# Four graph layers in one kernel: x W of layer 1 in halves, a different order at the first layer change, and other ends for layers 1 to 3

## The chip, the cores and the metric

The kernel runs on one core of a Trainium2 chip. The metric is the device time in microseconds (us), the median of several runs. The core has five engines with a queue each: TensorE (PE; its weight loads are shown as PEld), VectorE (DVE), ScalarE (ACT), GpSimd (POOL) and SyncE (SP), which here only issues transfers. An engine executes its queue in order and waits on semaphores.

## The reference

There are 4096 nodes, 256 features and a dense adjacency of 4096 x 4096 floats, of which most entries are zero. Each layer is followed by a residual sum and a layer norm over the features (LN).

```python
# layer 0: four heads of 64, masked where adj == 0
qkv = x @ Wqkv + bqkv
scores = q k^T / 8 + graph_bias * adj; masked to -1e9 where adj == 0
x = LN(x + (softmax(scores) @ v) @ Wout + bout)
# layer 1: one head, additive scores
Wh = x @ W;  e = leaky_relu((Wh @ a[:256])[:, None] + (Wh @ a[256:])[None, :], 0.2)
x = LN(x + softmax(e where adj > 0 or on the diagonal) @ Wh)
# layer 2
A = d[:, None] * adj * d[None, :]        # d = rowsum(adj) ** -0.5
x = LN(x + (A @ x) @ W2.T + b2)
# layer 3
x = LN(x + relu(A @ x @ W3))
```

## The kernel before, in words

A node block is 128 rows (a chunk, `NCH` = 32 of them); `xc` holds all chunks' rows, `mv` and `rstd` their mean, variance and reciprocal deviation. The order of instructions is written out by hand: `tc.manual_schedule()` keeps on each engine the order in which the program names them, and waits between engines follow from what each reads and writes.

**Layer 0** works in steps of 1024 columns; 64 units (32 row blocks by two head pairs) of 4 steps. Lists of what else is done in a step are kept in `plan` and `tail`. In the last steps the rows of layer 0's output, written to `x0_pre`, are loaded again in eight *parts* of four chunks (`load_part`), normalised (`norm_part`), written to `x0`, and turned into `turned_x` (`turn_part`). Parts 6 and 7 contain the last chunks and are turned last. `project_ed` makes from all turned parts the key scores `ed_b`. `project_w` (L132) multiplies a part with W and with W a: two halves, each 8 matmuls into one of the two double banks `sc[0]`, `sc[1]` of PSUM and one ScalarE copy into `store` (`wh`). The column next to Wh is the node's query score: `take_es` gathers it into `esd` on VectorE, and `spread_es` sends it through TensorE with a selecting matrix and back into `es_q`. At the end of layer 0 parts 0 and 1 are projected before parts 6 and 7 are turned.

**Layer 1** has 32 units (row blocks) of `NSB` = 4 passes of 32 rows, with the columns in four quarters over the partitions. `gat_step(t)` (L829) issues pass t of several stages: VectorE masks the edges (`mk`) and adds the key scores with a running maximum (`score`, L744 and L746), ScalarE adds the query score with the leaky slope (`leaky`, L759). When a unit's four maxima are there, ScalarE gathers them to one partition group (`gather_max`, L766), VectorE folds them (`fold_max`, L771), ScalarE spreads them (`spread_max`, L785). Then ScalarE takes the exponential (`expo`, L788), VectorE transposes (`turn`, L795), and TensorE multiplies with Wh (`attend`, L805): unit 0's `attend` starts in step 10 and needs all four turned passes of the unit. `finish` (L813) divides, adds to the row in `xc` and takes the statistics. In steps 0 to 5 each step also projects one of the parts 2 to 7; after that, in step 5, it takes and spreads the query scores of parts 2 to 7 and issues the eight loads of `xc`. SP's queue holds, in order, the edge masks of units 0 and 1, these eight loads, and the masks of unit 2 and later.

**Layers 2 and 3** multiply with the adjacency by a two-by-two scheme of seven products (Strassen's form). A step takes a pair of chunks c and c + 16 and a block of 512 columns from both halves: 7 products of 128 x 512 (L983), into seven PSUM banks `m0` to `m6`, accumulated over 16 steps; an eighth bank is tagged `y`. There are 4 column blocks a layer, so 128 steps. `load` (L938) brings two tiles of the adjacency by SP three steps ahead (4 buffers of two tiles); `sums` (L949) makes five sums or differences of them on VectorE one step ahead; `prepare` (L913) scales a pair's rows and makes five sums of them, during layer 2's first block, two steps ahead; layer 2's bias is added to the row by GpSimd there. After a block `keep` copies the seven banks out, `combine` makes four blocks of them, and `rows` (L1010) multiplies with W2 or W3, adds to `xc` and takes statistics, spread over later steps. `store` normalises the last layer's rows and writes the output. The end of the last block does all of this at once after the last product. Before layer 2's first step come `ln_rstd(0, NCH)`, `prepare(0, 0)` and `sums(0)`, which need the last unit's statistics.

## Time and profile before

| what | value |
| --- | --- |
| median of 3 runs (lowest, highest) | 2735.09 us (2731.63, 2736.67) |
| the profiled execution, its own time | 2734.35 us |
| its span | 2732.6 us |
| granted TensorE clock, mean | 0.992 |
| busy share of the span: PE, DVE, ACT, POOL | 98%, 80%, 60%, 14% |
| layer 1's last attend ends, layer 2's first product starts | 1875.3, 1881.5 us |
| adjacency load in layers 2 and 3, issue to landing, shortest, median, longest | 4.0, 5.1, 7.3 us |

A timeline row gives start, length, engine, line, operation and tiles, the number of instructions merged, and in brackets the engine's idle time before it with what released it; "issue" there means no releaser is shown. The same instruction can stand as two records: one product of 128 x 512 floats is two records of TensorE. Rows of stretches give, after the bounds and the length, the busy time of PE, PEld, DVE, ACT and POOL with the number of instructions, the granted clock (1.00 is full), the transfer engines' busy share and GB/s.

### The profile page before, as it was taken

How to read it: one execution, taken by the hardware profiler on the slowest of the kernel's cores; microseconds unless marked ns; L12 is line 12 of the kernel's file. 1: busy time of each engine (PE TensorE's matmuls, PEld its weight loads, DVE VectorE, ACT ScalarE, POOL GpSimd, SP SyncE). 2: the span in 40 equal slices, each digit the busy share in tenths (PEclk: the TensorE clock that was granted, in tenths of full speed). 3: DMA queues.
4: the chain of work that ended last, by engine and by line, in shares of the span. 5: the costliest groups of instructions: out<-in, count | busy, mean ns of one | idle time of the engine just before them, and what ended most of it. 6: DMA issues, size and time to landing. Idle time of an engine off the chain costs nothing.

```text
span 2732.6 us, 58953 instructions
## 1 busy us (share of the span) xinstructions
PE 2677.8 (98%) x23824; PEld 1836.4 (67%) x23824; DVE 2183.5 (80%) x3995; ACT 1647.8 (60%) x2675; POOL 379.4 (14%) x660
## 2 busy tenths in 40 slices
PE   8999999999999999999979999999999999999997
PEld 4777777777777777777768888885444444444443
DVE  4999999999999989999758888885866577676575
ACT  2899999999999999999857777771100001000000
POOL 1222232222222222223200000001200000000000
PEclk9999999999999999999999999999999999999998
DMA  6444444444444444444452222204554554555552
GB/s 146 94 96 96 89 94 95 92 96 94 88 96 95 92 90 96 97 89 91 143 160 73 77 78 77 74 20 133 179 159 155 174 159 153 168 175 161 183 174 69
DMA packets 679489, 312.35 MB, mean 114 GB/s; under 512 B 553520, under 2 KB 583600, under 8 KB 679216
## 3 DMA queue, kind: packets, MB, share of 16 engines
q1 hardware_dynamic: 655776, 265.10, 39.5%
q0 software_dynamic: 21632, 42.05, 4.3%
q8 instruction: 186, 3.05, 0.5%
q10 hardware_dynamic: 1808, 1.44, 0.2%
q14 instruction: 87, 0.71, 0.1%
HBM read 262.41 MB, written 46.07 MB: 113 GB/s over the span
## 4 chain that ended last, share of the span: by engine, by line
PE 94%; DVE 2%; DMA 2%; issue 1%; ACT 1%; SPq 0%; POOL 0%; DVEq 0%; POOLq 0%; ACTq 0%
PE m L983 28%; PE po L431 17%; PE sc L374 16%; PE po L805 16%; PE ptr L413 11%; PE py L1017 2%; PE pp L343 1%; PE pq L321 1%; PE pv L232 1%; PE pk L212 1%; DMA xt<-in_xT 0%; DMA mk<-edge 0%; DMA norm<-lt 0%; DMA x<-xs 0%; SPq L731 0%
## 5 line engine op out<-in xcount | busy, mean ns | idle before, releaser
L383 DVE CUSTOM_DVE_ANT_0 z<-sc,bias 128x1024 f32<-128x1024 f32 x512 | 606.0, 1221 | 50.9 <-PE sc L374 50.8
L399 ACT ACTIVATE z<-z,nm 128x1024 f32<-128x1024 f32 x512 | 590.6, 1154 | 0.0
L421 ACT COPY pt<-ptr 128x1024 f32<-128x1024 f32 x507 | 510.3, 1007 | 66.5 <-PE ptr L413 65.4
L431 PE MATMUL po<-pt,xc 128*64 128x128 f32 x8192 | 504.0, 276 | 0.0
L374 PE MATMUL sc<-store,qT 64*128 64x512 f32 x2048 | 502.9, 604 | 0.1
L805 PE MATMUL po<-store,pt 128*128 128x257 f32 x2048 | 447.2, 380 | 12.6 <-issue 12.6
L431 PEld LDWEIGHTS po<-pt,xc 128*64 128x64 f32 x8192 | 442.1, 137 | 17.5 <-DVE pt L419 0.2
L413 PEld LDWEIGHTS ptr<-ident,z 64*128 64x128 f32 x8192 | 322.9, 138 | 181.0 <-issue 86.9
L805 PEld LDWEIGHTS po<-store,pt 128*128 128x128 f32 x2048 | 389.1, 190 | 70.5 <-issue 12.7
L983 PE MATMUL m<-asum,ysum 128*128 128x512 f32 x768 | 356.7, 594 | 6.3 <-issue 6.3
L413 PE MATMUL ptr<-ident,z 64*128 64x64 f32 x8192 | 356.7, 225 | 5.1 <-ACT pt L421 3.7
L374 PEld LDWEIGHTS sc<-store,qT 64*128 64x128 f32 x2048 | 193.9, 189 | 115.6 <-issue 109.5
L983 PEld LDWEIGHTS m<-asum,ysum 128*128 128x128 f32 x768 | 146.2, 191 | 177.7 <-issue 160.8
L983 PE MATMUL m<-asum,store 128*128 128x512 f32 x512 | 263.3, 596 | 0.0
L983 PE MATMUL m<-a,ysum 128*128 128x512 f32 x512 | 246.0, 594 | 0.0
L989 ACT COPY e<-m 128x512 f32<-128x512 f32 x32 | 18.5, 585 | 351.3 <-PE m L983 351.3
L301 POOL DMA_DIRECT2D edge<-mk x256 | 143.1, 559 | 558.8 <-ACT mk L295 541.8
L759 ACT ACTIVATE z<-z,es_q 128x1024 f32<-128x1024 f32 x128 | 146.6, 1145 | 120.4 <-DVE mx L746 112.0
L952 DVE TENSOR_TENSOR asum<-a 128x512 f32<-128x512 f32 x128 | 88.0, 688 | 163.9 <-PE m L983 163.9
L284 DVE SCALAR_TENSOR_TENSOR bias<-rt,gb,u 128x512 f32<-128x512 f32 x256 | 194.2, 759 | 9.1
L795 DVE STREAM_TRANSPOSE pt<-z 128x1024 f32<-128x1024 f32 x128 | 158.0, 1236 | 41.7 <-PE po L805 41.7
L983 PEld LDWEIGHTS m<-asum,store 128*128 128x128 f32 x512 | 97.9, 191 | 123.2 <-issue 121.3
(122 smaller groups left out, 2601.3 us busy)
## 6 DMA issues: line engine op xcount, KB each, us to landing
a<-in_adjT SPq DMA_DIRECT2D x256, 512.0 KB, 5.1
raw<-in_adjT SPq DMA_DIRECT2D x512, 128.0 KB, 3.9
edge<-mk POOLq DMA_DIRECT2D x256, 128.0 KB, 2.4
mk<-edge SPq DMA_DIRECT2D x256, 128.0 KB, 2.9
xt<-in_xT SPq DMA_DIRECT2D x8, 512.0 KB, 5.1
xq<-in_xT SPq DMA_DIRECT2D x32, 128.0 KB, 3.6
xr<-in_x SPq DMA_DIRECT2D x32, 128.0 KB, 3.0
rb<-norm POOLq DMA_DIRECT2D x128, 32.0 KB, 2.4
```

Source lines behind the costliest of these rows:

```text
L284: nc.vector.scalar_tensor_tensor(self.bias[k][:, m0 : m0 + HT], rt, gb, u, ALU.mult, ALU.add)
L301: nc.gpsimd.dma_start(edge[self.ib * P : (self.ib + 1) * P, k * TS + m0 : k * TS + m0 + HT], mk)
L374: nc.tensor.matmul(ps[j][:, q * 512 : (q + 1) * 512], self.rows.qT[j * HD : (j + 1) * HD, self.pr, :], kT[j * HD : (j + 1) * HD, self.pr, ...
L383: nc.vector.tensor_tensor_reduce(z, ps[j], self.rows.bias[k], 1.0, NEG, ALU.add, ALU.max, self.mx[:, j, k : k + 1],)
L399: nc.scalar.activation(z, z, AF.Exp, bias=self.nm[:, j : j + 1], accum_out=self.ls[:, j, k : k + 1],)
L413: nc.tensor.transpose(pa[:, r, c, :], z[half, c * P : (c + 1) * P], ident[half, half])
L421: nc.scalar.copy(to, pa)
L431: nc.tensor.matmul(self.po[j * HD : (j + 1) * HD, 0:P], v_sb[:, ci, h * HD : (h + 1) * HD], self.pt[j][k][:, c, :], start=(ci == 0), stop= ...
L759: nc.scalar.activation(self.z[s], self.z[s], AF.Prelu, bias=self.eq[:, s : s + 1], alpha=SLOPE)
L795: nc.vector.transpose(self.pt[:, :, s, :], self.z[s].rearrange("p (b r) -> p b r", r=QB))
L805: nc.tensor.matmul(self.po[:, 0 : D + 1], self.pt[:, b, :, :].rearrange("p s i -> p (s i)"), wh[:, b, :], start=(b == 0), stop=(b == NBK - 1),
L983: nc.tensor.matmul(self.m[i], left, right, start=(c == 0), stop=(c == NP - 1))
```

## The change

**Between layers 0 and 1.** At the end of layer 0 only part 0 is projected before parts 6 and 7 are turned, and only its query scores are taken and spread. `project_w` now does one half, into a place it is given: `sc[0]`, `sc[1]` or `pm`, a third PSUM place. The fourteen other halves stand in steps 2 to 8 of layer 1, two or so a step; part 1's query scores are taken in step 2, those of parts 2 to 7 in step 9, the `xc` loads still in step 5. `leaky` comes two steps later, so that in ScalarE's queue a unit's gather comes before later leaky passes.

**Between layers 1 and 2.** The mask tiles' pool `bp` (7 tiles of 4 KB a partition) lives on and serves as the adjacency's buffers: two separate tiles a step. The loads of steps 0 to 2 are issued in the last steps of layer 1. The weights of layers 2 and 3 are loaded by SP in step 12 instead of by ScalarE. Chunks 0 to 30 are scaled, and pairs 0 and 1 prepared, into tiles of their own (`y_e`, `ysum_e`), six steps after the last pass's score; chunk 31's scale comes after the sums of step 0. The PSUM pool of layers 2 and 3 takes over its banks tile by tile.

**Steps of layers 2 and 3.** The products come in the order 2, 3, 0, 1, 4, 5, 6; products 2 and 3 read the adjacency tiles themselves, no sum. The difference that was one instruction over both tiles is two. The load for step t + 3 is issued after step t's second product.

**The end.** The last two steps are issued by product, both steps of a product together, in the order 2, 4, 0, 3, 6, 1, 5; blocks are combined in between, partly straight out of PSUM; rows are weighed from several banks; additions are shared between GpSimd and VectorE; and the output goes out in four transfers of two chunks.

```diff
-    def project_w(j):
-        xt = turned_x.pop(j)
-        for i in range(2):
-            pw = sc[i].rearrange("p (b e) -> p b e", b=2)
-            for b in range(2):
-                for cc in range(2):
-                    nc.tensor.matmul(
-                        pw[:, b, 0 : D + 1],
-                        xt[:, cc, 2 * i + b, :, :].rearrange("p a r -> p (a r)"),
-                        w_sb[:, cc, :],
-                        start=(cc == 0),
-                        stop=(cc == 1),
-                    )
-            bk = j * NSB + 2 * i
-            nc.scalar.copy(wh[:, bk : bk + 2, :], pw[:, :, 0 : D + 1])
+    def project_w(j, i, pw):
+        xt = turned_x[j] if i == 0 else turned_x.pop(j)
+        pw = pw.rearrange("p (b e) -> p b e", b=2)
+        for b in range(2):
+            for cc in range(2):
+                nc.tensor.matmul(
+                    pw[:, b, 0 : D + 1],
+                    xt[:, cc, 2 * i + b, :, :].rearrange("p a r -> p (a r)"),
+                    w_sb[:, cc, :],
+                    start=(cc == 0),
+                    stop=(cc == 1),
+                )
+        bk = j * NSB + 2 * i
+        nc.scalar.copy(wh[:, bk : bk + 2, :], pw[:, :, 0 : D + 1])
...
-            spread_es(0, 2 * NSB, ps_o.tile([P, 512], F32, tag="po0", name="pe"))
+            take_es(0, NSB)
+            spread_es(0, NSB, ps_o.tile([P, 512], F32, tag="po0", name="pe"))
...
                 (last_rstd,),
-                (project_w, 0),
-                (project_w, 1),
+                (project_w, 0, 0, sc[0]),
+                (project_w, 0, 1, sc[1]),
                 (norm_part, 6, NA - 1, NA),
                 (norm_part, 7, NA - 1, NA),
                 (turn_part, 6, True),
                 (turn_part, 7, True),
                 (project_ed, 6, NJ),
-                (take_es, 0, 2 * NSB),
                 (first_es,),
...
+    def load_last_weights():
+        nc.sync.dma_start(w2_sb, w2T.rearrange("(c p) e -> p c e", p=P))
+        nc.sync.dma_start(b2_b, b2.partition_broadcast(P))
+        nc.sync.dma_start(w3_sb, w3.rearrange("(c p) e -> p c e", p=P))
...
+    def prepare(p, layer):
+        dv = d2 if layer == 0 else d3
+        y, s = y_of(p), ysum_of(p)
+        for h in range(2):
+            ci = h * NP + p
+            ln_apply(xc[:, ci, :], xc[:, ci, :], ci)
+            nc.scalar.activation(y[:, h, :], xc[:, ci, :], AF.Copy, scale=dv[:, ci : ci + 1])
+            if layer == 0:
+                nc.gpsimd.tensor_tensor(xc[:, ci, :], xc[:, ci, :], b2_b, ALU.add)
+        nc.vector.tensor_tensor(
+            s[:, 1:3, :].rearrange("p a d -> p (a d)"), y[:, 0, :], y[:, 1, :], ALU.subtract
+        )
+        nc.vector.tensor_tensor(s[:, 3:5, :], y[:, :, 0:P], y[:, :, P : 2 * P], ALU.add)
+        nc.vector.tensor_tensor(s[:, 0, :], y[:, 0, 0:P], y[:, 1, P : 2 * P], ALU.add)
+    adj_t = {}
+    adj_s = {}
+    def load(t):
+        jb, c = divmod(t % T1, NP)
+        adj_t[t] = []
+        for k in range(2):
+            a = bp.tile([P, 2, BJ], F32, tag="bias", name=f"a{k}")
+            m0 = (k * NP + c) * P
+            nc.sync.dma_start(
+                a,
+                adjT[m0 : m0 + P, :].rearrange("p (h j i) -> p h j i", h=2, i=BJ)[:, :, jb, :],
+            )
+            adj_t[t].append(a)
...
-            u, s = at(t)
+            u, s = at(t - 2)
             if u:
                 u.leaky(s)
...
+        def more_es(j0, j1):
+            take_es(j0 * NSB, j1 * NSB)
+            spread_es(j0 * NSB, j1 * NSB, pm[:, 0:512])
...
+        filling = {}
+        halves = [(j, i) for j in range(1, NJ) for i in range(2)]
+        for t, n in ((2, 2), (3, 1), (4, 2), (5, 2), (6, 2), (7, 2), (8, 3)):
+            for _ in range(n):
+                j, i = halves.pop(0)
+                place = (sc[0], sc[1], pm)[(2 * j + i) % 3]
+                filling.setdefault(t, []).append((project_w, j, i, place))
+        filling[2].append((more_es, 1, 2))
+        filling[5].append((load_rows,))
+        filling[9] = [(more_es, 2, NJ), (degrees,)]
         with tc.manual_schedule():
             for t in range(n_t + NSB + 8):
                 gat_step(t)
-                if t + 2 < NJ:
-                    project_w(t + 2)
-                if t + 3 == NJ:
-                    take_es(2 * NSB, NBK)
-                    spread_es(2 * NSB, NBK, ps_o.tile([P, 512], F32, tag="pm", name="pe"))
-                    for j in range(NJ):
-                        nc.sync.dma_start(
-                            xc.rearrange("p (a j) e -> p a j e", j=NJ)[:, :, j, :],
-                            x0.rearrange("(a j p) e -> p a j e", p=P, j=NJ)[:, :, j, :],
-                        )
-                    nc.vector.reciprocal(d3, d3)
-                    nc.vector.reciprocal(d2, d2)
-                    nc.vector.tensor_scalar(sel, sel, -1.0, 1.0, ALU.mult, ALU.add)
-                    nc.vector.tensor_tensor(d2, d2, sel, ALU.mult)
+                if t == NJ + NSB:
+                    load_last_weights()
+                if n_t <= t < n_t + 3:
+                    load(t - n_t)
+                if t == n_t + NSB + 2:
+                    ln_rstd(0, NCH - 1)
+                    for p in range(NE):
+                        prepare(p, 0)
+                for f, *args in filling.get(t, ()):
+                    f(*args)
...
+        ps_m = l2.enter_context(
+            tc.tile_pool(name="l2ps_m", bufs=1, space=PSUM, reuse_waits="tile")
+        )
...
+            a0, a1 = adj_t[t]
             s = sp_.tile([P, 5, BJ], F32, tag="asum", name="asum")
-            nc.vector.tensor_tensor(s[:, 4, :], a[:, 0, 0, :], a[:, 1, 1, :], ALU.add)
-            nc.vector.tensor_tensor(s[:, 0:2, :], a[:, 0, :, :], a[:, 1, :, :], ALU.add)
-            nc.vector.tensor_tensor(s[:, 2:4, :], a[:, :, 0, :], a[:, :, 1, :], ALU.subtract)
+            nc.vector.tensor_tensor(s[:, 4, :], a0[:, 0, :], a1[:, 1, :], ALU.add)
+            nc.vector.tensor_tensor(s[:, 0:2, :], a0, a1, ALU.add)
+            nc.vector.tensor_tensor(s[:, 2, :], a0[:, 0, :], a0[:, 1, :], ALU.subtract)
+            nc.vector.tensor_tensor(s[:, 3, :], a1[:, 0, :], a1[:, 1, :], ALU.subtract)
...
+        order = (2, 3, 0, 1, 4, 5, 6)
...
+            def end(self, t0):
+                tt = nc.vector.tensor_tensor
+                e = wk.tile([P, 7, BJ], F32, tag="e", name="e", bufs=1)
+                hT = self.hT = wk.tile([P, 2, 2, BJ], F32, tag="hT", name="hT", bufs=1)
+                m, o0, o1 = self.m, e[:, 1, :], e[:, 5, :]
+                e0, e2, e3, e4 = (e[:, i, :] for i in (0, 2, 3, 4))
+                py = {}
+                def products(i):
+                    for t in (t0, t0 + 1):
+                        self.product(i, t)
+                    if i in (0, 2, 3, 4):
+                        nc.scalar.copy(e[:, i, :], m[i])
+                def weigh(n, tag, fs=(0, 1)):
+                    if n not in py:
+                        py[n] = ps_m.tile([P, 512], F32, tag=tag, name="py")
+                    for f in fs:
+                        self.weigh(n, py[n], f)
+                def onto_x(n):
+                    h, s = divmod(n, NSJ)
+                    ci = h * NP + self.jb * NSJ + s
+                    r = wk.tile([P, D], F32, tag="relu", name="relu")
+                    nc.scalar.activation(r, py[n][:, 0:D], AF.Relu, scale=d3[:, ci : ci + 1])
+                    eng = nc.vector if n > NSJ and n % 2 else nc.gpsimd
+                    eng.tensor_tensor(xc[:, ci, :], xc[:, ci, :], r, ALU.add)
+                def stats(n):
+                    h, s = divmod(n, NSJ)
+                    ci = h * NP + self.jb * NSJ + s
+                    ln_stats(wk, xc[:, ci, :], ci)
+                def put(h, engines):
+                    c0 = h * NP + self.jb * NSJ
+                    ln_rstd(c0, c0 + NSJ)
+                    ob = wk.tile([P, NSJ, D], F32, tag="ob", name="ob", bufs=2)
+                    for s in (0, 1, 3, 2):
+                        ln_apply(ob[:, s, :], xc[:, c0 + s, :], c0 + s, engines[s])
+                    for s, queue in ((0, nc.sync), (2, (nc.sync, nc.scalar)[h])):
+                        queue.dma_start(
+                            out[(c0 + s) * P : (c0 + s + 2) * P, :].rearrange(
+                                "(s p) e -> p s e", p=P
+                            ),
+                            ob[:, s : s + 2, :],
+                        )
+                products(2)
+                products(4)
+                products(0)
+                products(3)
+                tt(hT[:, 0, 1, :], e2, e4, ALU.add)
+                tt(o0, e0, e4, ALU.subtract)
+                tt(o1, e0, e2, ALU.add)
+                tt(o0, o0, e3, ALU.subtract)
+                products(6)
+                tt(hT[:, 0, 0, :], o0, m[6], ALU.add)
+                products(1)
+                tt(hT[:, 1, 0, :], m[1], e3, ALU.subtract)
+                tt(o1, o1, m[1], ALU.subtract)
+                weigh(0, "m2")
+                weigh(1, "m4")
+                products(5)
+                tt(hT[:, 1, 1, :], o1, m[5], ALU.subtract)
+                weigh(2, "m0")
+                weigh(3, "m3")
+                for n in range(NSJ):
+                    onto_x(n)
+                    stats(n)
+                for n, tag in zip(range(NSJ, 2 * NSJ), ("m6", "m1", "m5", "y")):
+                    weigh(n, tag, (0,))
+                put(0, [nc.vector] * NSJ)
+                for n in range(NSJ, 2 * NSJ, 2):
+                    for i in range(n, n + 2):
+                        weigh(i, None, (1,))
+                        onto_x(i)
+                    stats(n)
+                    stats(n + 1)
+                put(1, [nc.vector] * (NSJ - 1) + [nc.gpsimd])
...
-        ln_rstd(0, NCH)
-        for t in range(3):
-            load(t)
         with tc.manual_schedule():
-            prepare(0, 0)
             sums(0)
-            prepare(1, 0)
+            ln_rstd(NCH - 1, NCH)
             blk = None
             for t in range(n_all):
                 layer, tl = divmod(t, T1)
                 jb, c = divmod(tl, NP)
                 if c == 0:
                     blk = Block(layer, jb)
-                if t + 3 < n_all:
-                    load(t + 3)
                 if t + 1 < n_all:
                     sums(t + 1)
-                for i in range(7):
+                if t >= n_all - 2:
+                    if t == n_all - 1:
+                        blk.end(t - 1)
+                    continue
+                for n, i in enumerate(order):
                     blk.product(i, t)
-                    if i == 2:
+                    if n == 1 and t + 3 < n_all:
+                        load(t + 3)
+                    if n == 2:
                         do(t, "mid")
                 del adj_t[t], adj_s[t]
-                if layer == 0 and jb == 0 and c + 2 < NP:
-                    prepare(c + 2, 0)
+                if layer == 0 and jb == 0 and c + NE < NP:
+                    prepare(c + NE, 0)
...
```

## The prediction

> **What bounds the kernel now.** First the chain of waits by engine, then TensorE's timeline across each change of layer, then what ScalarE, VectorE and the granted clock did in the holes found there.
>
> ```profile
> PE 94%; DVE 2%; DMA 2%; issue 1%; ACT 1%; SPq 0%; POOL 0%; DVEq 0%; POOLq 0%; ACTq 0%
> ```
>
> TensorE sets the end. The change removes no product of layers 1 to 3, so only TensorE's holes can pay. Between 1430 us and the end TensorE waits 13.9 us in all (6.3 + 2.6 + 2.1 + 2.1 + 0.8), and before 1430 one hole of 12.6 us stands out. The first hole, between layers 0 and 1:
>
> ```profile
> 1409.16 3.74 PE L139 MATMUL sc<-w_sb,xt 128*128 128x257 f32 x16 [0.23 <-ACT store L147]
> 1414.41 1.04 PE L157 MATMUL pe<-esd,pick 128*128 128x24 f32 x8 [1.51 <-DVE esd L150]
> 1428.09 12.24 PE L805 MATMUL po<-store,pt 128*128 128x257 f32 x47 [12.64 <-issue]
> ```
> ```profile
> 1405.50 0.59 ACT L147 COPY store<-sc 128x514 f32<-128x514 f32 x1 [1.15 <-PE sc L139]
> 1406.11 0.60 ACT L766 COPY mx<-mx 32x4 f32<-32x4 f32 x3
> 1406.74 0.17 DVE L771 TENSOR_REDUCE mr<-mx 32x4 f32<-32x16 f32 x1 [7.33 <-ACT mx L766]
> 1409.61 1.28 ACT L788 ACT_TABLE_LOAD   x1
> 1410.91 1.15 ACT L788 ACTIVATE z<-z,nm 128x1024 f32<-128x1024 f32 x1
> 1414.08 0.18 DVE L150 COPY esd<-store 128x24 f32<-128x24 f32 x1 [5.21 <-ACT store L147]
> ```
> ```profile
> 1420.00:1425.00 5.00, 0.00 (x0) 0.00 (x0) 4.90 (x10) 4.38 (x8) 0.00 (x0) 0.50 0.34 105
> 1430.00:1435.00 5.00, 5.00 (x21) 4.21 (x20) 4.93 (x9) 4.40 (x7) 0.00 (x0) 0.83 0.27 88
> ```
>
> The copies of x W (L147) stand in ScalarE's queue before unit 0's gather of maxima (L766), each waiting for TensorE. VectorE idles 7.33 us for that gather and 5.21 us for the last copy, so the first exponential starts at 1410.91 and the first attend at 1428.09. The windows (seventh number after the bounds: granted clock) show 0.50 in the hole and 0.83 just after.
>
> The second hole and the tail:
>
> ```profile
> 1875.31 0.17 DVE L815 RECIPROCAL rc<-po 128x1 f32<-128x1 f32 x1 [12.54 <-PE po L805]
> 1880.66 0.68 DVE L952 TENSOR_TENSOR asum<-a 128x512 f32<-128x512 f32 x1
> 1881.54 2.04 PE L983 MATMUL m<-asum,ysum 128*128 128x512 f32 x2 [6.27 <-issue]
> ```
> ```profile
> 2705.14 0.68 DVE L999 TENSOR_TENSOR hT<-e 128x512 f32<-128x512 f32 x1
> 2717.57 5.44 PE L1017 MATMUL py<-w_sb,hT 128*128 128x256 f32 x14 [0.77 <-DVE hT L1008]
> 2725.50 2.67 DVE L124 TENSOR_SCALAR ob<-xc,mv,rstd 128x256 f32<-128x256 f32 x8
> 2726.91 1.67 SPq L1040 DMA_DIRECT2D out_x<-ob  x2
> ```
>
> After the last attend the last chunk's statistics, the scale of all chunks, the first pair's preparation and its sums run one after another before a product starts. At the end everything from L999 on follows the last product, ending about 2705.3; the span ends at 2732.6: 27.3 us.
>
> **Part 1, layers 0 to 1.** I place the new order by hand with the rows' durations. Up to 1379.06 nothing moves. Then only x W of part 0 stands before the last two turns: 8 matmuls instead of 16, 3.5 us of the 7.22 us row. The turns, the last key scores and ed_b come 3.5 us earlier: ed_b at 1387.9 where before it was 1391.4, and unit 0's first score behind it. A half of x W is 1.74 us on TensorE and 0.59 on ScalarE, a score step 1.65 on VectorE (0.42 + 1.23), a leaky pass or exponential 1.1 on ScalarE, a turn 1.24.
>
> Step 2 adds a wait: VectorE takes the scores of part 1 and waits for copy (1,1) on ScalarE, then for TensorE's spread (0.95 us; the row for 24 columns took 1.04). Behind it on VectorE stands the fourth score, which ends at 1397.1 instead of 1394.4; for it waits the gather. The gather ends at 1398.2 (before: 1406.7), since the leaky pass of step 4 and the later copies now stand behind it. ScalarE's order from there: leaky 1.15, spread of the folded maxima 0.6, two copies 1.15, table load 1.28, so the first exponential starts at 1402.4 (before: 1410.9). Steps 5 to 7 are one exponential, one leaky pass and two copies, 3.3 to 3.5 us each. Step 8 has the next gather, the fourth exponential (ends 1414.0), a leaky pass, a spread, and three copies until 1417.4. Step 9's taking of the remaining scores waits for these copies, its spread ends at 1418.9, and the attends stand behind it. VectorE's fourth turn ends at 1417.6, not later. So attends start at 1418.9: 9.2 us earlier. TensorE has its 14 halves (24.4 us) in those 29 us, and the clock doesn't fall: 47 attend records took 12.24 us where 35.59 us held 163 at full clock (0.218 each), 2.0 us lost, now saved. Sum 11.2.
>
> One rule bears on it: the Trainium skill, "ScalarE: Activation LUTs", section "What ACT_TABLE_LOAD costs", puts a switch at 2.66 us, a load of about 1.28 and a drain of 1.38. The row shows a load of 1.28 directly behind a copy and an activation 1.30 after it starts. With the row attends start at 1418.9, with the page 1420.3, a gain of 9.8. I take the row.
>
> Unknown is how TensorE and ScalarE interlock over three places. If each of five steps slips by 1 us this part gives 6; if the copies hide fully, 14. I take 11.2, the sum of rows.
>
> SP's queue keeps its order here: masks of units 0 and 1, eight row loads, masks of unit 2. Those row loads wait for the last parts' writes, SP gets past them at 1390.2 as before, and unit 2's first four masks issue at once; they are needed at about 1408.
>
> **Part 2, layers 1 to 2.** Loads of steps 0 to 2 go on SP from about 1850 in both versions. The scale of 31 chunks needs unit 30's statistics (ready 1862.8), and two preparations of 2.7 to 3.0 us fit beside unit 31's attend (14.0 us); cover gone, they'd cost 6. VectorE then finishes unit 31 in 1.4 us and makes four sums: 0.60, 1.14, 0.60, 0.60 from start to start. The first two products need no sum: 2 x 0.86 us. The third waits for the first sum (1.4 + 0.7 against 1.7), with the next about 0.8 us of stall in all. Before: 6.27 us of hole, then 244 product records in 107.0 us where 0.429 each (174 in 74.67) gives 104.7, 2.3 lost to the half clock and the sums. Gain 6.27 + 2.3 - 0.8 = 7.8, between 5 (the sums late for two steps) and 8.5.
>
> The three weight loads move from ScalarE's queue to SP at step 12 behind unit 3's masks: 1.4 us of issue, hidden by a lead of many microseconds.
>
> **Part 3, every step of layers 2 and 3.** The split of one 1.21 us difference into two of 0.68 adds 0.07 us to VectorE (2 x 0.60 against 1.13). In the preparing steps VectorE takes 5.89 of TensorE's 6.01 us; it becomes 5.96 and stays hidden. Cover gone, 14 steps lose under 1 us. A pair of loads now goes out after the second product of a step instead of at its start, the second half needing that step's own tile. It's wanted two steps later, 11 us on, and landings took 4.0 to 7.3 us. The two stalls of 2.1 us at the layer switch stay. Zero.
>
> **Part 4, the end.** The last two steps start about 2693.3 (28 records x 0.429 before 2705.3). By product instead of by step, the products end at 1.7, 3.4, 5.2, 6.9, 8.6 and 10.3 us after that; copies and combining run beside them. Four halves of combined rows are ready at 9.5, 11.1 and, behind the seventh product (13.7), 14.6. Rows 0 to 3 are weighed by 15.5, the rest by 18.9 (0.86 a row). Row 3's relu, GpSimd's addition (0.8, from L923) and statistics end at 17.7, the first half's output starts at 20. Of the second half: VectorE adds row 5 at 20.5, statistics and row 7 end at 23.3, the scale takes 0.9, three applications 1.1: 25.4. Output landing adds 4.4 as before (2728.2 to 2732.6). End at 29.8 instead of 39.3: 9.5.
>
> Against it speaks the Trainium skill, "SBUF — State Buffer", section "SBUF: two separate sides": VectorE and GpSimd share ports under an exclusive lock, and the loser waits for the whole instruction. The row agrees in kind, not size: L928 took 0.94 beside GpSimd and 0.42 without, 0.5 more. Six additions at 0.8 would take 4.8, leaving 4.7; by the row, with two on the path, 1 us, leaving 8.5. I take 9: most additions run while VectorE waits for relu. Range 5 to 11.
>
> **Sum.** 11.2 + 7.8 + 9 = 28.0. Span 2732.6 becomes 2704.6. The profiled execution took 2734.35, so 1.75 lies around the span, giving 2706.4; the median, 2735.09, is 0.74 above that execution: 2707.
>
> **Rivals.** (a) *All three gains add*: 2707, chance 0.76.
>
> (b) *A part pays less*. The chain of waits names a mask load, landing at 1406.06, ahead of the gather. If the gather truly needed it, 8 of part 1's us would go: 2715. Against it: ScalarE's copy ended at 1406.09 and the gather began at 1406.11, so its own queue explains it. Or the tail's ports and the interlock take 5 to 8. Together 0.16, about 2714.
>
> (c) *Slower: layers 2 and 3 become load-bound*. Seven half tiles replace eight, so half of each pair goes out later. There are 128 steps; above 28 / 128 = 0.22 us a step the gains are gone. It decides once landings pass about 11 us; 0.35 a step gives 2752. The longest, 7.3, speaks against it. 0.05.
>
> (d) *It doesn't do what it says*: attends start earlier but VectorE, 89% busy in layer 1, can't keep up, and the tail hits GpSimd: about 2731. Against it: VectorE needs 13.4 of the unit's 14.0 us (four steps of 2.95, a fold, a finish), and no wait of TensorE is seen after 1428. 0.03.
>
> **The numbers.** Changes under 0.2% (5.5 us) can't be told from none. Faster: (a) and (b), 0.92; same 0.03; slower 0.05. The summed lower ends of parts 1, 2 and 4 are 16 us, upper 33; eight times in ten: 2701 to 2718.
>
> **What would show it.** First attend near 1419 at full clock, x W between the leaky passes, no hole over 3 us there; VectorE's gather wait well under 7 us. First product of layer 2 within 0.2 us of the last attend, then under 1 us of stall. Step cadence of 6.01 us. The last two steps' start to span end: about 30 us. Wrong if SP shows loads waiting beyond a step, or if the hole only moves from before the attends to between the x W halves.

## The result and the profile after

| | before | after |
| --- | --- | --- |
| median of the runs (lowest, highest), us | 2734.90 (2731.63, 2736.67) | 2705.74 (2704.63, 2708.07) |
| after / before, 95% interval | | 0.9897 (0.9882 to 0.9911) |
| the profiled execution, its span, us | 2734.35, 2732.6 | 2704.96, 2703.2 |
| first attend starts, us | 1428.09 | 1417.82 |
| layer 2's first product starts, us | 1881.54 | 1863.06 |
| the last two steps start, us | 2693.18 | 2673.82 |

The kernel is 29.2 us faster by the medians, 29.4 by the two spans; 2707 was predicted. The last three rows divide the span into four stretches, and the gain with it: 10.3 us before the first attend, 8.2 from there to layer 2's first product, 0.9 from there to the last two steps, 10.0 in the end.

In the changed kernel the lines have moved: x W is L139 and its copy L147; score L803 and L805, leaky L818, gather L825, exponential L847, attend L864; a sum L990 to L993, a product L1026, the row of layer 2 L1074, the rows of the end L1097 to L1125.

First the chain that ended last, by engine, of the changed kernel's page:

```profile
PE 95%; DMA 1%; DVE 1%; ACT 1%; issue 1%; SPq 0%; POOL 0%; POOLq 0%; ACTq 0%; DVEq 0%
```

TensorE still sets the end, with 95% instead of 94%. Then the timeline of the first layer change, VectorE, ScalarE and TensorE (start, length, engine, line, tiles, and in brackets the idle time before):

```profile
1387.49 0.42 DVE L623 COPY ed_b<-ped 128x256 f32<-128x256 f32 x1 [0.55 <-PE ped L612]
1393.77 0.17 DVE L150 COPY esd<-store 128x4 f32<-128x4 f32 x1 [1.25 <-ACT store L147]
1395.09 0.17 DVE L164 COPY es_q<-pm 128x16 f32<-128x16 f32 x1 [1.15 <-PE pm L157]
...
1396.93 0.59 ACT L147 COPY store<-sc 128x514 f32<-128x514 f32 x1 [2.15 <-PE sc L139]
1397.54 0.60 ACT L825 COPY mx<-mx 32x4 f32<-32x4 f32 x3
1401.05 1.28 ACT L847 ACT_TABLE_LOAD   x1
1402.34 1.15 ACT L847 ACTIVATE z<-z,nm 128x1024 f32<-128x1024 f32 x1
1405.38 1.16 ACT L847 ACTIVATE z<-z,nm 128x1024 f32<-128x1024 f32 x1
1408.41 1.17 ACT L847 ACTIVATE z<-z,nm 128x1024 f32<-128x1024 f32 x1
...
1416.90 1.07 PE L157 MATMUL pm<-esd,pick 128*128 128x24 f32 x8 [0.89 <-DVE esd L150]
1417.82 1.55 PE L864 MATMUL po<-store,pt 128*128 128x257 f32 x6
```

The gather starts at 1397.54 instead of 1406.11, 0.02 us after the copy ahead of it in ScalarE's own queue. The hole of 12.64 us before the attends has become one of 0.89, before the last spread. It has not moved between the halves of x W: from layer 0's last output product to the first attend, TensorE's waits sum to 3.3 us instead of 15.0. Two windows of the changed kernel (granted clock is the seventh number after the bounds):

```profile
1420.00:1425.00 5.00, 5.00 (x25) 4.36 (x24) 4.93 (x9) 4.34 (x7) 0.00 (x0) 1.00 0.07 23
1430.00:1435.00 5.00, 5.00 (x25) 4.36 (x24) 4.83 (x11) 3.63 (x4) 0.00 (x0) 1.00 0.34 105
```

TensorE is full in both, and the clock is 1.00 where it had been 0.50 and 0.83. At the second change, TensorE's and VectorE's timeline:

```profile
1863.06 1.88 PE L1026 MATMUL m<-a,ysum_e 128*128 128x512 f32 x4
1864.65 0.69 DVE L990 TENSOR_TENSOR asum<-a,a 128x512 f32<-128x512 f32 x1
1865.49 1.10 PE L1026 MATMUL m<-asum,ysum_e 128*128 128x512 f32 x2 [0.56 <-DVE asum L990]
```

The first two products (four records) follow the last attend without a gap, the third waits 0.56 us for its sum. From there to the end TensorE's waits are these (engine, line, releaser: us in total, times, longest):

```profile
PE py L1057 <- DVE xc L1074: 2.3, 1, 2.3
PE m L1026 <- DVE asum L990: 0.6, 1, 0.6
```

The end, from the start of the last two steps (the timeline of the changed kernel, TensorE, VectorE and GpSimd):

```profile
2673.82 1.88 PE L1026 MATMUL m<-a,ysum 128*128 128x512 f32 x4
2687.57 5.34 PE L1057 MATMUL py<-w_sb,hT 128*128 128x256 f32 x24
...
2692.20 2.20 DVE L125 TENSOR_SCALAR ob<-xc,mv,rstd 128x256 f32<-128x256 f32 x4
2692.39 1.53 POOL L1111 TENSOR_TENSOR xc<-xc,relu 128x256 f32<-128x256 f32 x2 [1.56 <-ACT relu L1109]
2694.32 0.41 DVE L1111 TENSOR_TENSOR xc<-xc,relu 128x256 f32<-128x256 f32 x1
2697.90 1.22 DVE L125 TENSOR_SCALAR ob<-xc,mv,rstd 128x256 f32<-128x256 f32 x3
```

From 2673.82 to the span's end it is 29.4 us, against 39.4. Weighing fills TensorE until 2692.9. What follows is VectorE's until 2699.1, then the last transfer.

### The profile page after: what moved, and what is told of

Read it like the earlier page. It is cut to its first block, busy times and chain, and to the rows that moved or that the text cites. A ratio compares the mean times of both kernels' runs of the same rounds, so it can differ in the third digit from the quotient of the medians.

```text
span 2703.2 us, 59041 instructions
## 1 busy us (share of the span) xinstructions
PE 2670.2 (99%) x23832; PEld 1833.4 (68%) x23832; DVE 2188.5 (81%) x4119; ACT 1637.0 (61%) x2677; POOL 385.6 (14%) x668
## 3 DMA queue, kind: packets, MB, share of 16 engines
q10 hardware_dynamic: 1392, 1.05, 0.1%
## 4 chain that ended last, share of the span: by engine, by line
PE 95%; DMA 1%; DVE 1%; ACT 1%; issue 1%; SPq 0%; POOL 0%; POOLq 0%; ACTq 0%; DVEq 0%
PE m L1026 28%; PE po L431 17%; PE sc L374 17%; PE po L864 16%; PE ptr L413 11%; PE py L1057 2%; PE pv L232 1%; PE pp L343 1%; PE pq L321 1%; PE pk L212 1%; DMA mk<-edge 0%; DMA norm<-lt 0%; DMA x<-xs 0%; DMA bqk_sb<-in_bqk 0%; DMA xt<-in_xT 0%
## 5 line engine op out<-in xcount | busy, mean ns | idle before, releaser
L864 PE MATMUL po<-store,pt 128*128 128x257 f32 x2048 | 445.4, 380 | 0.0
L864 PEld LDWEIGHTS po<-store,pt 128*128 128x128 f32 x2048 | 387.9, 189 | 57.1
L1026 PE MATMUL m<-asum,ysum 128*128 128x512 f32 x672 | 324.9, 593 | 0.0
L1026 PEld LDWEIGHTS m<-asum,ysum 128*128 128x128 f32 x672 | 128.0, 191 | 160.6 <-issue 141.0
L990 DVE TENSOR_TENSOR asum<-a,a 128x512 f32<-128x512 f32 x128 | 88.0, 688 | 156.9 <-PE m L1026 156.9
L1026 PE MATMUL m<-a,ysum 128*128 128x512 f32 x448 | 212.3, 597 | 0.0
L1026 PE MATMUL m<-asum,store 128*128 128x512 f32 x448 | 210.6, 593 | 0.0
L278 DVE STREAM_TRANSPOSE rt<-raw 128x512 f32<-128x512 f32 x256 | 179.9, 703 | 0.3 <-issue 0.3
L805 DVE CUSTOM_DVE_ANT_0 z<-mk,ed_b 128x1024 f32<-128x1024 bf16 x128 | 156.9, 1226 | 4.6
```

Source lines behind the costliest of these rows:

```text
L278: nc.vector.transpose(rt.rearrange("p (b r) -> p b r", r=QB), self.raw_now[:, half * nb : (half + 1) * nb, :],)
L805: nc.vector.tensor_tensor_reduce(z, m, ed_b, 1.0, NEG, ALU.add, ALU.max, self.mx[:, 0, s : s + 1],)
L864: nc.tensor.matmul(self.po[:, 0 : D + 1], self.pt[:, b, :, :].rearrange("p s i -> p (s i)"), wh[:, b, :], start=(b == 0), stop=(b == NBK - 1),
L1026: nc.tensor.matmul(self.m[i], left, right, start=(c == 0), stop=(c == NP - 1))
```

## The experiments

Executions of the same code don't all reach the first layer change at the same time: layer 0's last output product (the last L343) started between 1378.3 and 1382.5 us in the thirteen profiles. Everything about part 1 is therefore counted from that product. The two rows are from groups by line, of the kernel before and of the changed one; the last number of "first and last start" is the one meant:

```profile
L343 PE MATMUL pp<-wout_sb,oT x256: 378/379/431, 133.8 to 1378.8; 128*64 128x256 f32 x128
```
```profile
L343 PE MATMUL pp<-wout_sb,oT x256: 378/379/431, 134.0 to 1379.3; 128*64 128x256 f32 x128
```

So the first attend comes 49.3 us after it before the change and 38.5 us after it with the change: 10.8 us earlier, of which the profiled pair shows 10.3, since its layer 0 happened to end 0.5 us later. All eight profiles that contain the whole of part 1 give 38.5 us within 0.1, so a difference of 1 us counted this way can be read from one execution. The experiments without a median below were executed once, and only their traces are read.

### Part 1 alone

The kernel before, with part 1 and nothing else.

```diff
-    def project_w(j):
+    def project_w(j, i, pw):
...
-            u, s = at(t)
+            u, s = at(t - 2)
             if u:
                 u.leaky(s)
...
+        for t, n in ((2, 2), (3, 1), (4, 2), (5, 2), (6, 2), (7, 2), (8, 3)):
+            for _ in range(n):
+                j, i = halves.pop(0)
+                place = (sc[0], sc[1], pm)[(2 * j + i) % 3]
+                filling.setdefault(t, []).append((project_w, j, i, place))
```

> The kernel before with part 1 of the change alone (x W in halves over three places, last parts turned first, leaky passes two steps later). Theory, each part's gain is TensorE's hole closed and the parts add: attends of layer 1 start near 1418 instead of 1428.1 and take 445.3 us instead of 447.2, nothing after that changes, span 2720.4 against 2732.6, median 2722.7. Rival, the later holes swallow part of an earlier start: layer 1 to 2 hole longer than 6.3 us, span 2725 or more.

TensorE's timeline of this kernel:

```profile
1416.79 5.46 PE L805 MATMUL po<-store,pt 128*128 128x257 f32 x24
...
1868.48 2.04 PE L1000 MATMUL m<-asum,ysum 128*128 128x512 f32 x2 [6.28 <-issue]
```

Median 2721.56 us, 0.9958 (0.9942 to 0.9975) of the kernel before, whose median beside it was 2732.94; span 2719.5. The first attend is again 38.5 us after layer 0's last product. The hole of 6.28 at the next layer change is untouched, and the stretch from layer 2's first product to the end is 851.0 us, as before (851.1). Part 1's gain stays where it arises: it adds to the others.

### The clock by itself

The kernel before, with 26 products of no use in its hole of 12.6 us. They keep TensorE busy and bring nothing forward.

```diff
                     spread_es(2 * NSB, NBK, ps_o.tile([P, 512], F32, tag="pm", name="pe"))
+                    warm = ps_o.tile([P, 512], F32, tag="pm", name="warm")
+                    for _ in range(26):
+                        nc.tensor.matmul(
+                            warm[:, 0 : D + 1], ident, w_sb[:, 0, :], start=True, stop=True
+                        )
```

> The kernel before with 26 matmuls more in the hole before layer 1's attends (52 records of 257 columns, some 11.5 us; their result is not used), so that TensorE isn't idle. Theory, the slow first attends are the halved clock's: attends start at 1428.1 as before but all 2048 records take 445.3 us instead of 447.2, span 2730.7, granted clock 1.00 in all of 1415 to 1440. Rival, they are slow for another reason (weights or transposed tiles late): 447.2 as before, span 2732.6.

Its timeline and a window:

```profile
1416.26 12.95 PE L871 MATMUL warm<-w_sb,ident 128*128 128x257 f32 x52
1429.08 3.28 PE L805 MATMUL po<-store,pt 128*128 128x257 f32 x14
```
```profile
1430.00:1435.00 5.00, 5.00 (x24) 4.36 (x23) 4.93 (x9) 3.88 (x7) 0.00 (x0) 1.00 0.29 84
```

The attends run at clock 1.00 from the first one. From the first attend to layer 2's first product it is 451.67 us instead of 453.45, with the same hole of 6.3 in both: the half clock behind the long hole cost 1.8 us. Part 1 alone gives the same by another way, 451.69. In the kernel before the clock is 0.50 until 1431.7, 3.6 us into the attends, and half of that is the 1.8. The span fell by 2.1, to 2730.5. The first attend started 1.0 later: layer 0 ended 0.7 later, and the useless products ran 0.3 over the hole. The stretch behind layer 2's first product was 1.3 shorter, and that is the clock too: it stayed full behind the wait at the switch from layer 2 to 3 (1.7 us) and was lowered for less of the end (0.6), but for longer behind the hole of 6.3 (1.0 lost).

### Inside part 1: three single edits undone

First, the leaky passes of unit 0 and 1 put back into their old steps, ahead of the gather and the copies.

```diff
-            u, s = at(t - 2)
-            if u:
+            u, s = at(t if t < 2 * NSB else t - 2)
+            if u and t not in (2 * NSB, 2 * NSB + 1):
                 u.leaky(s)
```

> The changed kernel with the leaky passes of the first two units at their old step (from step 10 on two steps later again). Theory, ScalarE's order sets the start of the attends: four leaky passes and the copies stand before the first gather again, gather some 2 us later than 1398.1, attends start at 1420 to 1421 instead of 1417.8, span 2705 to 2706.5. Rival, TensorE's own x W work fills the time and sets the start: 1418 to 1418.5, span within 0.7 of 2703.2.

```profile
1395.21 0.17 DVE L150 COPY esd<-store 128x4 f32<-128x4 f32 x1 [2.24 <-ACT store L147]
...
1420.14 5.03 PE L864 MATMUL po<-store,pt 128*128 128x257 f32 x22
```

VectorE's wait for part 1's copy, which stands behind three leaky passes here, grows from 1.25 to 2.24 us. The first attend is 40.3 us after layer 0's last product: 1.8 us later. The span is only 0.6 longer, 2703.8: layer 0 ended 0.5 later in this execution, and the layer switch gave back 1.7, as shown below. By the span alone the rival would have won.

Second, two places instead of three for the halves of x W.

```diff
-                place = (sc[0], sc[1], pm)[(2 * j + i) % 3]
+                place = sc[i]
```

> The changed kernel with the halves of x W put into the two old PSUM places only. Theory, the third place lets TensorE run ahead of ScalarE's copies: with two, each step's pair of halves (3.5 us) starts only after the pair before is copied, so steps 4 to 8 take about 4.2 us instead of 3.05, attends start near 1423, span near 2708.5. Rival, the sum of TensorE's work sets the start: 1418 to 1419, span below 2704.5.

```profile
1416.16 0.17 DVE L830 TENSOR_REDUCE mr<-mx 32x4 f32<-32x16 f32 x1 [4.05 <-ACT mx L825]
...
1423.43 1.77 PE L864 MATMUL po<-store,pt 128*128 128x257 f32 x7
```

Products and copies now take turns. Unit 1's maxima come late, VectorE's wait for them rising from 2.74 to 4.05 us, and the first attend is 40.9 us after layer 0's last product: 2.4 later. The size expected was twice that. The span, 2708.8, contains another 3.2 us of a layer 0 that ended late in this execution, which an unaltered kernel showed too (below); that it lies near the 2708.5 expected is chance.

Third, part 1 projected before the last turns again, as in the kernel before.

```diff
                 (project_w, 0, 0, sc[0]),
                 (project_w, 0, 1, sc[1]),
+                (project_w, 1, 0, sc[0]),
+                (project_w, 1, 1, sc[1]),
                 (norm_part, 6, NA - 1, NA),
...
-        filling[2].append((more_es, 1, 2))
```

> The changed kernel with part 1 projected before the last two turns again and its query scores taken and spread together with part 0's; step 2's halves and its taking and spreading are gone. Theory, turning the last parts first brings ed_b 3.5 us forward, but VectorE's wait in step 2 gives 2.7 of it back: attends start within 1 us of 1417.8. Rival, the 3.5 us are worth 3.5: attends start at 1421.3, span 2706.7.

```profile
1398.23 0.60 ACT L827 COPY mx<-mx 32x4 f32<-32x4 f32 x3 [1.53 <-DVE mx L807]
1401.55 3.68 PE L139 MATMUL pm<-w_sb,xt 128*128 128x257 f32 x8 [2.21 <-ACT store L147]
...
1419.20 6.12 PE L866 MATMUL po<-store,pt 128*128 128x257 f32 x27
```

The first attend is 39.5 us after layer 0's last product: 1.0 later. `ed_b` comes 3.5 us later, but the trip of step 2, with its waits of 1.25 and 1.15 us on VectorE, is gone. Turning the last parts first is thus worth 1.0 of the 3.5 us that it moves. The gather (first row) waits here for VectorE's score, not for ScalarE's copies. The eight products behind the wait of 2.21 took 3.68 us, where other groups of eight took 1.90; this slow stretch is in the 1.0, and there is more on it in the last section.

### Part 2 without its cover

The changed kernel with the scale and the two preparations behind the last attend.

```diff
-                if t == n_t + NSB + 2:
-                    ln_rstd(0, NCH - 1)
-                    for p in range(NE):
-                        prepare(p, 0)
...
+            ln_rstd(0, NCH)
+            prepare(0, 0)
             sums(0)
-            ln_rstd(NCH - 1, NCH)
+            prepare(1, 0)
```

> The changed kernel with the scale of all chunks and the preparation of pairs 0 and 1 back behind the last attend; loads ahead, PSUM taken over by tile, order of products as changed. Theory, the early preparation carries part 2: TensorE idles 4 to 5 us before the first product (1.4 finish, 0.85 scale, 0.75 application, 1.3 until the first sums of rows), the clock halves after it, the last two steps start 5 to 6.5 us later, span 2708.2 to 2709.7 against 2703.2. Rival, the loads and the PSUM takeover carry it: less than 1 us later.

```profile
1868.40 3.78 PE L1022 MATMUL m<-a,ysum_e 128*128 128x512 f32 x4 [4.45 <-DVE ysum_e L748]
```

TensorE waits 4.45 us, and the four records behind it take 3.78 us instead of 1.88. The first product starts 4.6 us after the attends end (1418.55 + 445.24). From there to the end it is 840.1 us; executions with a full clock at the layer switch, as this one, otherwise took 838.4 (shown below), so the slow start cost 1.7 more than the changed kernel's stall. Cover gone, the price is 4.6 + 1.7 = 6.3 us, which the prediction had put at 6. The span is 2708.5, as expected. The order of products, the earlier loads and the banks taken over tile by tile stayed in; what each of them is worth was not tried.

### Part 4 undone

The changed kernel with the old kind of end: all seven banks copied, then combined, then weighed.

```diff
-                if t >= n_all - 2:
-                    if t == n_all - 1:
-                        blk.end(t - 1)
-                    continue
...
+            for h in range(2):
+                blk.combine(h)
+                for n in range(h * NSJ, (h + 1) * NSJ):
+                    blk.rows(n, f"m{n % 7}")
+            block_rstd(NJB - 1)
+            for h in range(2):
+                blk.store(h)
```

> The changed kernel with the end of the last block as before: last two steps by step, copies out, combining, rows, one scale, two output transfers. Theory: from the start of the last two steps to the span's end 39.4 us instead of 29.4, span 2713.2. Rival, GpSimd's additions slow the new end so that it is worth under 5 us: span below 2708.

Its TensorE waits after 2660 us:

```profile
PE py L1057 <- DVE hT L1047: 2.6, 1, 2.6
PE py L1057 <- DVE hT L1044: 2.1, 1, 2.1
PE py L1057 <- DVE hT L1051: 1.3, 1, 1.3
```
```profile
2697.28 4.98 PE L1057 MATMUL py<-w_sb,hT 128*128 128x256 f32 x14 [1.29 <-DVE hT L1051]
```

Three waits for combined blocks are back; the changed kernel has none there. From layer 2's first product to the end it is 849.5 us instead of 840.1: the end is worth 9.4 us by this, 10.0 by the comparison with the kernel before. The difference is the clock in the old end: the last fourteen records of weighing take 4.98 us here (granted clock 0.63 in the first 2.5 us) and took 5.44 in the kernel before (0.50). So the new order itself is worth 9.4. The span of 2711.8 is 1.4 under the expected one: 0.6 for this, and 0.8 because layer 0 ended earlier here than in the changed kernel's trace.

### What VectorE and GpSimd cost each other in the end

All eight additions of the end on VectorE.

```diff
-                    eng = nc.vector if n > NSJ and n % 2 else nc.gpsimd
+                    eng = nc.vector
```

> The changed kernel with all eight additions of the last block's end on VectorE, so that GpSimd works in the end only for its one application. Theory (the row's price: a GpSimd operation costs VectorE about half a microsecond where they run side by side): the first half's four applications fall from 2.20 to about 1.6 us, VectorE gets six additions of 0.40 us, of which only the two of the second half and about one of the first lie on its path; from the start of the last two steps to the span's end it is 29.4 to 29.9 us (29.4 in the changed kernel), span 2703 to 2706. Rival (the two engines shut each other out for whole operations[...]): six GpSimd additions of 0.8 us fewer for six VectorE ones of 0.4 us, so the end falls by 1.5 to 3 us, to 26.5 to 28 us.

```profile
2694.65 1.38 DVE L125 TENSOR_SCALAR ob<-xc,mv,rstd 128x256 f32<-128x256 f32 x4
...
2700.20 1.14 DVE L125 TENSOR_SCALAR ob<-xc,mv,rstd 128x256 f32<-128x256 f32 x3
```

The same four applications took 2.20 us beside two of GpSimd's additions and take 1.38 without: 0.41 for each. But the first addition stands behind the last combination in VectorE's queue, and all four of the first half now lie on its path, so the applications start 19.3 us after the last two steps instead of 18.4; with two more additions in the second half the end takes 30.3 us. That is longer than either theory said. Against the rival the answer is clear: here one of GpSimd's additions, of 0.77 us each, costs VectorE about half its length, not all of it, and moving the work away doesn't pay.

### The layer switch, and an unaltered kernel beside it

Counted from layer 2's first product to the end, executions with the new end fall into two groups 1.7 us apart: 840.1 in the changed kernel and with two places, 838.4 with early leaky passes and with part 1 first. The wait of 2.3 us for L1074, where layer 2 hands over to layer 3, is in all of them. The edit below removes it: it writes the block's rows one step later and puts off the last six preparations, two by six steps and four by three, so that VectorE has less to do in those steps.

```diff
+                    late = int(layer == 0 and jb == NJB - 1)
                     for n in range(2 * NSJ):
-                        at_step(t + 2 + n // 2, ("mid", "end")[n % 2], blk.rows, n)
-                    at_step(t + 2 + NSJ, "mid", block_rstd, jb)
+                        at_step(t + 2 + late + n // 2, ("mid", "end")[n % 2], blk.rows, n)
+                    at_step(t + 2 + late + NSJ, "mid", block_rstd, jb)
...
-                            at_step(max(t + 2 + NSJ + s, free), "end", prepare, p, 1)
+                            at_step(max(t + 2 + NSJ + s, free + 6 * (p > 9)), "end", prepare, p, 1)
```

> The changed kernel with less of VectorE's work in the two steps after layer 2's last block: rows one step later, preparations of pairs 10 to 15 six steps after their first allowed step. Theory, TensorE's 2.3 us wait for a row there is VectorE's backlog, and the half clock after it costs another 1.6: both go, span 2699.3, median 2701.8. Rival, the backlog shows again some steps on: span 2701.5 to 2703.2.

Median 2702.75 (2700.22 to 2704.33), 0.9887 (0.987 to 0.9903) of the kernel before. From layer 2's first product to the end it is 835.8 us. Then the changed kernel, unaltered, and this one, in one comparison on the same chip:

> The changed kernel once more, unaltered, beside the next one on the same chip, for the 1.7 us by which executions of the same code differ between the last attend and the span's end. Theory (the wait of 2.3 us at the switch from layer 2 to 3 starts a stretch of half clock in some executions and not in others): this time is 840.1 us where the windows around 2285 show a clock below 0.8, and 838.4 us where they show 1.00. Rival (the difference comes from elsewhere, the loads or the end): it doesn't go with the clock there. Median 2705 to 2707 us.

> The kernel that writes the last block's rows one step later and makes the last six preparations six steps later at the switch from layer 2 to 3, on the same chip as the changed kernel, in five rounds. Theory (it saves the wait of 2.3 us and the half clock after it, 4.3 us in all against the changed kernel's first trace, 2.3 against an execution at full clock): 835.8 us from the last attend to the end, median 2.5 to 4.5 us below the changed kernel's of this call. Rival (the work put off is late elsewhere in other executions, and the first figure was luck): within 1 us of the changed kernel's median.

Windows behind the switch, first of the unaltered changed kernel in this repetition, then of the kernel with early leaky passes, then of the kernel with the edit:

```profile
2285.00:2290.00 5.00, 2.67 (x7) 1.40 (x7) 4.21 (x11) 0.91 (x2) 0.00 (x0) 0.87 0.00 0
2290.00:2295.00 5.00, 5.00 (x13) 2.57 (x12) 4.90 (x11) 0.00 (x0) 0.00 (x0) 0.79 0.54 167
```
```profile
2285.00:2290.00 5.00, 2.92 (x9) 1.82 (x10) 4.21 (x12) 0.91 (x2) 0.00 (x0) 1.00 0.00 0
```
```profile
2285.00:2290.00 5.00, 5.00 (x17) 2.88 (x16) 2.13 (x5) 0.00 (x0) 0.00 (x0) 1.00 0.60 208
```

The unaltered kernel shows 840.1 us and a lowered clock (0.87 and 0.79), as its first trace did (0.66 in the window 2285 to 2290). The executions with 838.4 us show 1.00 there. So behind the same wait of 2.3 us a stretch at half clock sometimes follows and sometimes not, and the stretch costs 1.7 us; what decides is in the last section. Where the wait is gone, all windows from 2275 to 2300 show 1.00, in both profiles of this edit. Which of its two changes counts was not tried. Layer 0 also ended 2.8 us later in this repetition than in the first trace (last L343 at 1382.1), with no edit at all, and the first attend was again 38.5 us after it.

| in the same comparison | median, lowest to highest, us | of the kernel before |
| --- | --- | --- |
| changed kernel | 2706.65, 2704.49 to 2707.77 | 0.9896 (0.9881 to 0.9911) |
| with the spread switch | 2702.18, 2701.16 to 2703.85 | 0.9882 (0.9866 to 0.9899) |

The version with the spread switch is 4.5 us faster by the medians, and the two sets of runs don't overlap: it beats both kernels. The traces give 4.3 us for it (840.1 to 835.8), or 2.6 against an execution whose clock stayed up.

## Why the prediction was right

The likeliest case, that all three gains add, is what happened, and the mechanism of each part is the one predicted. That the sum came within 1.4 us is in part luck: part 1 gave more than its term, part 2 less, and chance took 0.5. The terms against the measured ones, in us:

| term of the sum | predicted | measured | from |
| --- | --- | --- | --- |
| part 1, attends earlier | 9.2 | 10.8 | 49.3 and 38.5 after layer 0's last product |
| layer 0 ended later by chance | – | -0.5 | last L343 at 1378.8 and 1379.3 |
| part 1, clock | 2.0 | 1.8 | 453.45 and 451.67, the hole kept busy |
| part 2 | 7.8 | 7.3 | 451.67 to 445.24, and 811.64 to 810.76 |
| part 3 | 0 | 0 | within part 2's second pair |
| part 4 | 9 | 10.0 | 39.4 and 29.4, of which 0.6 is clock in the old end |
| sum | 28.0 | 29.4 | spans 2732.6 and 2703.2 |

**Part 1.** By the times of the trace the order placed by hand held to the first exponential: predicted at 1402.4, measured at 1402.34, with the gather ending at 1398.14 against 1398.2. But this layer 0 ended 0.5 us late, so that agreement hides an error of 0.5: counted from layer 0's last product, `ed_b` came 4.0 us earlier (8.6 behind it instead of 12.6), where 3.5 had been placed. In the kernel before, products of another part's x W ran between the last key scores on TensorE, and VectorE waited 1.12 us for these scores instead of 0.55:

```profile
1390.97 0.42 DVE L623 COPY ed_b<-ped 128x256 f32<-128x256 f32 x1 [1.12 <-PE ped L612]
```

The larger step that was mis-sized is the one after the first exponential, "one exponential, one leaky pass and two copies, 3.3 to 3.5 us each". The exponentials start 3.04 and 3.03 us apart. The row's length of 1.15 us had been added up, but on ScalarE the next instruction starts 1.05 us after it, so lengths overstate a sequence by about 0.1 us for each instruction. The copies ended at 1416.6 instead of 1417.4 and the attends started at 1417.8 instead of 1418.9. The order of the leaky passes (1.8), the third place (2.4) and the last parts first (1.0) each carry part of the gain. If they add, which no run shows, they make 5.2 of the 10.8; x W spread over steps in halves, the rest, was not tried by itself. The last of the three is small, because the wait that the prediction saw in step 2 takes back most of its 3.5 us. The table load of 1.28 us, with the exponential 1.29 after its start, agrees with the row that was taken, not with the longer price of the Trainium skill ("ScalarE: Activation LUTs", "What ACT_TABLE_LOAD costs").

**Part 2.** The first product followed the last attend directly. The stall was 0.56 + 0.28 + 0.07 = 0.9 us (from the starts 1865.49, 1866.63 and 1868.42, two products taking 0.86), against 0.8. The preparations were hidden, and cost 6.3 us when they weren't. Of the shortfall of 0.5, 0.4 lies in the first steps of layer 2: they gained 1.1 us where 1.5 (2.3 - 0.8) had been put (up to the row behind the switch's wait it was 422.6 us before and 421.7 after, less waits of 2.14 and 2.34). The longer wait at the switch adds 0.2, and the hole gave 0.2 more than its 6.27. The slow stretch behind that wait cost both kernels the same. Here are the row behind the wait and the next one, of the kernel before and of the one with the products of no use, whose clock stayed full there:

```profile
2304.11 1.13 PE L1017 MATMUL py<-w_sb,hT 128*128 128x256 f32 x4 [2.14 <-DVE xc L1026]
2309.35 1.03 PE L1017 MATMUL py<-w_sb,hT 128*128 128x256 f32 x4
```
```profile
2304.27 1.13 PE L1022 MATMUL py<-w_sb,hT 128*128 128x256 f32 x4 [2.13 <-DVE xc L1031]
2307.81 1.03 PE L1022 MATMUL py<-w_sb,hT 128*128 128x256 f32 x4
```

They start 5.24 us apart in the first, 3.54 in the second: 1.7. In the changed kernel's trace it is 5.24 as well.

**Part 3.** A step stayed at 6.01 us, and TensorE waited for no transfer; loads landed in 4.7 us (median) instead of 5.1. Two things in this step were wrong. Of the "two stalls of 2.1 us at the layer switch" only one lies there; the other belongs to the old end, as the waits of the kernel with the old end show. And the one that stays was called zero because it doesn't change, but removing it was worth 4.3 us, 2.6 where the clock had stayed up.

**Part 4.** The sum by rows was good: VectorE was to add row 5 at 20.5 us after the last two steps' start and did so at 20.50; the last applications were to end at 25.4 and ended at 25.3. Contention was priced at 1 us by the row, of which the final 9 charged half, and took about 0.8, all in one place (2.20 against 1.38 us). It was inside those times, so other rows had been a little too long. The last transfer landed in about 4.1 us where 4.4 had been assumed. The 4.8 us estimated from the exclusive lock of the Trainium skill ("SBUF — State Buffer", "SBUF: two separate sides") by whole additions weren't seen.

**The rivals.** The changed kernel's chain names a mask load again, landing at 1397.50, 0.04 us before the gather, so the name alone settles nothing. But in twelve of the thirteen profiles the gather starts 0.02 to 0.03 us after the copy ahead of it ends, whenever that is, and in the thirteenth (part 1 first) it waits for VectorE's score: the mask load does not set its start. That layers 2 and 3 become bound by loads is refuted by TensorE's two waits, neither on a transfer. That VectorE can't keep up in layer 1 is refuted by windows with TensorE busy for 5.00 of 5.00 us.

## What to carry to other kernels

When a queue executed in order holds up another engine, move the work that nobody waits for behind the instruction that somebody waits for; here it closed a hole of 12.6 us without removing a single product. Place the new order by hand with the distances between starts of the rows, not with their lengths: the lengths put the first attend 1.1 us too late. Count small differences from an origin inside the trace. And when the large holes are closed, price the small one again: a wait of 2.3 us was worth up to 4.3.

## What the runs showed of the hardware

A wait of 2.1 to 2.3 us can halve TensorE's clock for 3.4 us. Of the eleven profiles that have the wait at the switch from layer 2 to 3, seven show it (the next weighing 5.24 us later) and four don't (3.54). What decides, by these eleven, is where the wait lies. The stretches at half clock last 3.413 us or a multiple of it in every trace (but for the last, which the end cuts off), and they start and end on one grid of that step: in the kernel before they start at 1418.07, 1878.87, 2305.54 and 2708.31, which are 135, 125 and 118 steps apart. Two steps of the grid around the wait, first of the changed kernel, then of the one with early leaky passes (its grid carried over from another slow stretch, which starts at 2695.86):

```profile
2282.30:2285.71 3.41, 1.07 (x5) 0.87 (x5) 3.27 (x8) 0.00 (x0) 0.00 (x0) 1.00 0.00 0
2285.71:2289.13 3.42, 3.42 (x5) 1.35 (x4) 2.70 (x8) 0.91 (x2) 0.00 (x0) 0.50 0.02 5
```
```profile
2282.84:2286.26 3.42, 1.91 (x5) 0.57 (x3) 3.35 (x6) 0.00 (x0) 0.00 (x0) 1.00 0.20 76
2286.26:2289.67 3.41, 2.58 (x8) 1.63 (x9) 2.69 (x9) 0.91 (x2) 0.00 (x0) 1.00 0.00 0
```

In the first the whole wait falls into one step, TensorE is idle for 2.34 of 3.41 us, and the next step runs at 0.50. In the second the wait is split, 1.51 and 0.83, and the clock stays up. In the seven slow executions one step holds 1.99 to 2.34 us of idle time at the switch, in the four others at most 1.81. Half of 3.4 us is the 1.7 that the stretch costs. The wait of 2.21 us with part 1 first lies in one step too, and the eight products behind it take 3.68 us instead of 1.90. Idle time is not all that counts: in the kernel with the products of no use, a step with 1.51 us of it (1412.37 to 1415.78) also precedes a slow one; behind its wait stand short products of 24 columns. The Trainium skill ("TensorE: Matmul & The Clock Gate", "Part 1: The HAM clock gate") gives windows of about 3.4 us that run freely, which the grid agrees with, and a lowered clock after an idle window; here a window idle for 2 us of its 3.4 was enough.

Layer 0 ended up to 4.2 us apart between profiles of kernels that don't differ there. Without an origin behind it, the experiment with two places would have read as 5.6 us instead of 2.4.
